# Q and K products over two pairs at a time, and a mask written over logits in PSUM, in a two-layer graph network

## The chip, the core and the metric

The kernel runs on one core of one Trainium2 chip. The time of a run is the device time of that core in microseconds, from the start of the execution to its end. The kernel before takes 2388.6 us (median of 3 runs, 2387.88 to 2389.69).

A core has five engines that run their own streams of instructions in order: PE (TensorE, matrix products, with the weight loads shown apart as PEld), DVE (VectorE), ACT (ScalarE), POOL (GpSimd) and SP (SyncE, which here issues nearly all DMAs). They wait for each other through semaphores.

## The reference

There are 128 independent batches. Each has x with 128 rows and 512 columns in float32 and a 128x128 integer adjacency. Two layers follow each other:

```python
# layer 0: attention with 8 heads of 64 columns, masked by the adjacency
q, k, v = x @ Wq + bq, x @ Wk + bk, x @ Wv + bv
logits = einsum('bqhd,bkhd->bhqk', q, k) / 8
attn = softmax(where(adj > 0, logits, -1e9))
x = layernorm(x + relu(einsum('bhqk,bkhd->bqhd', attn, v) @ Wo + bo))
# layer 1: graph attention with one head
Wh = x @ W
e = leaky_relu((Wh @ a1)[:, None] + (Wh @ a2)[None, :], 0.2)
x = layernorm(x + elu(softmax(where(adj == 0, -1e9, e)) @ Wh))
```

All of it is float32.

## The kernel before

**Pairs.** The work goes by pairs of batches: pair p holds batches 2p and 2p+1, so there are 64 pairs. Everything of a pair is a step with a name (`qk0`, `logits`, `mask_logits1`, `w_c11` and so on), a small function that emits its instructions.

**Products with a weight.** Four weights are applied: Wq and Wk (together `wqk`, their output kept with features on partitions), Wv, Wo and W. The two batches of a pair and the two halves of the contraction make a two-by-two block form, and the products are made with seven block products in place of eight (`PRODUCTS`), with sums of blocks made ahead: `weight_sums` once for each weight, `left_sums` for each pair (steps `x_sums`, `o_sums`, `z_sums`, four operations on POOL each). The seven block products accumulate in three PSUM banks A, B, C, and between them ACT or DVE read the banks and combine (steps `_p1`, `_p6`, `_c11`, `_p7`, `_c22`, `_c21`, `_c12`). For V, O and W the weight is the moving operand, 256 columns wide (`rows_product`, L531). For Q and K the weight block is stationary and x is the moving operand, 128 columns (the rows of one batch or of one sum) wide (`columns_product`, L542): 4 feature chunks by 2 contraction chunks, 8 matrix instructions for each block product. A float32 matrix instruction appears in the trace as two records on PE and two on PEld.

**Attention.** `logits(p)` (L791) makes the logits of both batches of the pair, one after the other: 8 heads each, contraction over 64 rows, two heads side by side on the two halves of the array's rows. The result of a batch fills two PSUM banks (pool `ps_att`, two buffers). POOL has filled an SBUF tile `pr` with -1e9 (`fill_logits`, L799; two buffers); DVE copies the logits over it where the mask is one (`mask_logits`, L803), which sets the PSUM buffer free, and takes the negated row maximum from `pr` (L808). ACT takes the exponential in place with its row sum (L814, 8 instructions with a reading of the accumulator each), DVE inverts the sums, ACT scales (L824), DVE transposes 32x32 blocks into `prb` (L837), and SP writes `prb` to HBM and reads it back in the other order into `prT` (L850, L859: one DMA and four). `mix_values(b)` (L869) multiplies with V: outputs of 64 partitions, two heads side by side on the two halves of the array's columns. In layer 1, `mix_nodes` (L997) multiplies the attention with x on the whole array.

**x.** `load_blocks(p)` loads both batches of a pair in 32x32-friendly order into `xb`, `x_transpose` (L586, DVE) transposes a batch into `xT` (four buffers), and `load_x` loads the plain rows for the residual (two buffers).

**The order.** Nothing is scheduled at run time. `PLAN` gives each step a due time within a pair, `PERIOD` is added for each later pair, and `ENDS` shifts steps in the first and last pairs; all steps are sorted by that time and emitted in that order, and each engine's stream is what results. Only the order counts, the times themselves are never waited for. `GOING` adds empty products (`keep_going_late`, L1086) at a few places near the end. The last pair has shorter ways: transposes on PE instead of DMA, W and O products in plain form (L713), and work on DVE that is otherwise POOL's (`side_engine`).

Of the kernel before, what the change touches and what calls it, by code (L numbers as in the profile page):

```python
# [17 lines left out]
PERIOD = 81.828156  # L18
PLAN = dict(
    load_blocks=-169.2518, sums_qk=-116.3679, sums_v=-101.8019, x_transpose0=-86.1319, x_transpose1=-79.7504,  # L20
    sums_o=-74.3987, x_sums=-35.3263, qk0=-32.7245, qk1=-27.0361, qk4=-25.8081, qk_p1=-24.9029, qk_p1q=-24.7398,
    qk_p6=-23.2631, qk2=-21.6091, qk_c11=-19.491, qk3=-17.7869, fill_logits1=-14.9084, qk_p7=-13.984,
    load_adj=-12.9311, qk_c22=-9.2149, v0=-8.4276, qk5=-7.2181, qk6=-7.1845, qk_c21=-5.2279, v_p1=-4.9633,
    fill_logits0=-4.7424, v1=-3.3064, qk_c12=-2.1207, v_p6=-1.6137, v2=-1.3636, mask=-0.6144, logits=0.0,
    mask_logits0=2.1354, v3=3.4342, v_c11=5.3342, sums_fold1=5.6709, max_logits0=7.2929, v4=7.8473, v_p7=10.5301,
    v_c22=11.0507, v5=11.2435, mask_logits1=11.7414, v6=12.2065, v_c12=13.0477, v_c21=13.7783, max_logits1=14.0311,
    exp_logits0=14.9455, sums_fold_t1=29.5382, sum_logits0=36.5851, sums_fold0=38.0441, sums_fold_out1=39.3173,
    sums_fold_t0=41.2777, norm_logits0=49.133, exp_logits1=53.5487, weights_t0=54.0334, sum_logits1=54.4411,
    norm_logits1=57.8787, sums_fold_out0=60.6355, weights_out0=64.5346, weights_t1=66.3279, weights_out1=76.2441,
    weights_in0=76.8757, mix_values0=83.0319, weights_in1=83.7749, mix_values1=84.6403, mix_values_out0=86.1105,  # L30
    mix_values_out1=88.1579, sums_w=91.2147, o_sums=95.3864, o0=95.754, load_x1=104.4976, o_p1=109.4377,
    o1=117.6112, o4=119.0515, load_x0=121.4079, o_p6=122.4978, fill_edges=124.7475, o_p1l=126.1443, o3=126.686,
    o2=130.451, o_p7=131.8715, o_c11=134.1407, o_c22=134.3039, o5=134.9475, o6=135.0912, o_c21=136.1861,
    o_c12=136.4788, residual00=137.0927, stats00=138.5041, mean00=144.6048, residual01=145.8591, stats01=147.1796,
    rstd00=149.175, mean01=149.4786, shift00=151.0198, rstd01=151.4241, norm00=152.5598, shift01=155.6025,
    norm01=156.4175, edge_term10=156.4398, edge_term11=160.2785, edge_blocks=166.4223, edge_term01=170.0896,
    edge_term00=172.7812, edge_row=180.5447, edge_sums=180.8282, edge_leaky=182.3038, edge_mask=194.0334,
    edge_max=194.7432, edge_exp=203.146, edges_t=205.2742, edges_t_out=211.9867, edges_t_in=212.3358,
    mix_nodes1=225.9448, mix_nodes_out1=227.9602, edge_norm=229.8523, mix_nodes0=230.0102, mix_nodes_out0=234.9992,
    z_sums=244.2793, w0=261.4366, w1=262.5692, w_p1=262.5723, w_p6=263.0005, w2=264.29, w3=266.6663, w_c11=267.2067,  # L40
    w4=268.1639, w_p7=273.5439, w_c22=276.1897, w5=278.0097, w_c21=278.1222, w6=279.5606, w_c12=283.7313,
    elu_exp1=292.9307, elu_exp0=299.1665, elu_low1=300.2511, elu_low0=311.7113, elu_max1=315.4258,
    elu_max0=317.7063, tail_exp=321.2554, residual10=327.3123, residual11=342.0393, stats10=351.2992,
    mean10=362.4035, stats11=364.5992, mean11=365.5761, rstd10=371.9636, shift10=402.4303, finish0=423.5343,
    rstd11=447.2308, shift11=460.7052, finish1=468.0909, store0=483.1352, store1=502.9344, tail_max=616.0679,
    tail_sum=623.954, tail_norm=855.4691)
# [3 lines left out]
        load_x0=-307.1688, qk_p1=-220.4916, qk6=-209.3085, qk5=-208.2226, x_transpose0=-184.4755,  # L50
        fill_logits0=-182.6106, qk_p1q=-177.9107, qk2=-176.9987, x_transpose1=-174.505, qk0=-168.3877,
        qk_c11=-153.0006, qk1=-151.2359, qk_c21=-146.2578, qk3=-135.3339, qk_c12=-133.7443, fill_logits1=-117.9224,
        tail_exp=-115.7058, qk_c22=-114.2801, qk4=-109.4256, mask=-96.5947, qk_p6=-95.0022, tail_max=-93.0873,
        v1=-92.9444, v0=-88.8394, logits=-85.7847, mask_logits0=-83.9035, v_p1=-82.6878, v2=-81.4129, v_p6=-81.3346,
        norm_logits0=-79.0358, max_logits0=-75.6452, x_sums=-73.0228, qk_p7=-72.4402, v3=-72.1557,
        sum_logits0=-71.2808, weights_t0=-65.6654, mask_logits1=-65.4693, v_p7=-63.2932, v4=-62.9197,
        load_adj=-62.6051, exp_logits1=-62.2906, v_c11=-60.6749, v5=-59.9717, v_c22=-57.2207, exp_logits0=-53.7987,
        max_logits1=-49.1528, finish0=-37.8374, weights_out0=-36.1445, v6=-35.9047, stats11=-34.6264,
        tail_sum=-33.7386, v_c12=-32.1388, v_c21=-30.8773, weights_in0=-29.626, store0=-26.7007, shift01=-26.6327,
        weights_in1=-25.8217, edge_term01=-24.2286, rstd01=-23.1277, stats01=-22.9131, o_c11=-22.584,  # L60
        mean01=-22.0409, residual01=-21.8677, sum_logits1=-20.5549, residual11=-20.3839, o2=-19.79,
        weights_out1=-18.3632, o_p1l=-17.629, shift10=-17.1551, o3=-17.1166, norm01=-16.4822, o_p6=-16.4536,
        o_c22=-15.7638, o_c21=-15.4619, o5=-15.3535, o_p7=-15.3253, o1=-15.1127, o4=-14.5824, elu_exp1=-13.7949,
        weights_t1=-13.7748, norm_logits1=-11.4151, o6=-11.2616, mix_values0=-10.9462, mix_values1=-10.1036,
        o_p1=-9.8975, edge_row=-9.4454, edge_mask=-9.2922, elu_low1=-9.2535, residual00=-9.2117, o_c12=-8.661,
        w_c22=-8.624, elu_max1=-7.7019, w_p7=-7.4203, mix_values_out1=-7.2999, mix_values_out0=-7.2036,
        edge_term11=-6.8813, edge_sums=-5.9449, w5=-4.9426, w_c12=-4.5009, w0=-4.39, w_p1=-4.1709, mean10=-3.9319,
        w6=-3.836, w_c21=-3.5995, w2=-3.414, w_c11=-3.3202, w1=-2.7704, load_x1=-2.4908, edge_blocks=-1.6838,
        w4=-1.5143, edges_t_out=-1.3526, o0=-1.2931, w3=-0.7222, rstd10=-0.6162, edge_term00=-0.5897, w_p6=-0.2046,
        o_sums=0.3336, edges_t=0.5007, edge_exp=1.3317, edge_leaky=2.1715, rstd00=2.3393, mix_nodes1=2.6091,  # L70
        stats10=2.6585, edge_max=2.9908, stats00=4.202, finish1=5.0102, mix_nodes_out1=5.0231, mean00=5.5742,
        edges_t_in=5.865, mix_nodes0=5.8668, shift11=6.2663, mix_nodes_out0=6.8887, edge_term10=7.4794,
# [220 lines left out]
def tile_two_graph_layers(ctx: ExitStack, tc: tile.TileContext, x, adj, wq, bq, wk, bk, wv, bv, wo, bo, w, a, out,  # L293
# [13 lines left out]
    DH = D // H  # L307
    HALF = D // 2
    n_pair = n_batch // 2
    NEG = -1.0e9  # L310
    EPS = 1e-5
    ALPHA = 0.2

# [858 lines left out]
```

## Time and profile before

| quantity | value |
| --- | --- |
| time, median of 3 | 2388.6 us |
| span of the profiled execution, first to last instruction | 2386.0 us |
| PE busy | 2365.4 us (99%), 17762 records |
| PEld busy | 2148.5 us (90%) |
| DVE busy | 1904.3 us (80%), 3891 instructions |
| ACT busy | 1539.8 us (65%), 5501 instructions |
| POOL busy | 1399.1 us (59%), 1984 instructions |
| DMA | 276 MB, mean busy share 45% of 16 engines |
| mean granted TensorE clock | 0.999 |

The span ends 2.6 us short of the median time. A busy PE means that a matrix instruction is in it; the ends of matrix instructions are modelled, so that the true rate is read from the starts of instructions that follow each other. In a timeline a row gives the start, the time from the first start to the last end, engine, line, operation, tile written and tiles read, shapes and the number of records; what is in brackets is the idle time of the engine just before and what ended it. The chain of waits is followed back from the last instruction, at each step to what released it.

### The profile page before, as it was taken

To read this page: it belongs to the slowest core of one execution; us is meant where nothing else is said; L and a number is where in the kernel's file an instruction comes from. 1 tells how busy PE (TensorE), PEld (TensorE's weight loads), DVE (VectorE), ACT (ScalarE), POOL (GpSimd) and SP (SyncE) were. 2 spreads that over 40 slices of the span, in tenths; PEclk is the share of its full clock that TensorE was granted. 3 is DMA by queue.
4 is the path that set the end of the run, shared out by engine and by line. 5 is a ranking of instruction groups with operands and counts; after the bars stand their busy time and mean duration, and the time that the engine had idled before them with its cause. 6 is when DMAs were issued, how large, how long until landed. Compare 5 with 4: busy or idle time off the path is not lost.

```text
span 2386.0 us, 51849 instructions
## 1 busy us (share of the span) xinstructions
PE 2365.4 (99%) x17762; PEld 2148.5 (90%) x17762; DVE 1904.3 (80%) x3891; ACT 1539.8 (65%) x5501; POOL 1399.1 (59%) x1984
## 2 busy tenths in 40 slices
PE   8999999999999999999999999999999999999997
PEld 8998999989989999999899999998998999989985
DVE  6778888788788887887887878878878788787787
ACT  4665676666766756666667567666675675666664
POOL 3355655656656656566566565565665655656557
PEclk9999999999999999999999999999999999999999
DMA  7444444535444445454444443443544444445342
GB/s 188 118 98 102 127 109 116 131 90 129 123 99 130 110 115 131 94 126 127 94 130 114 110 131 96 129 127 89 130 121 102 131 108 117 122 96 138 102 103 78
DMA packets 340981, 276.18 MB, mean 116 GB/s; under 512 B 126192, under 2 KB 288496, under 8 KB 340720
## 3 DMA queue, kind: packets, MB, share of 16 engines
q1 hardware_dynamic: 339504, 271.57, 45.3%
q8 instruction: 142, 2.33, 0.4%
q10 hardware_dynamic: 1216, 1.31, 0.2%
q14 instruction: 119, 0.97, 0.1%
HBM read 156.77 MB, written 107.74 MB: 111 GB/s over the span
## 4 chain that ended last, share of the span: by engine, by line
PE 95%; ACT 1%; DMA 1%; DVE 1%; POOL 1%; issue 0%; SPq 0%; POOLq 0%; ACTq 0%; DVEq 0%
PE pBqk L542 14%; PE pCqk L542 9%; PE pAqk L542 9%; PE pACw L531 9%; PE pACo L531 9%; PE pACv L531 9%; PE pBv L531 7%; PE pBw L531 7%; PE pBo L531 7%; PE s L791 5%; PE po L869 5%; PE pz L997 5%; ACT pr L814 1%; ACT pr L824 0%; DMA ejr<-ej 0%
## 5 line engine op out<-in xcount | busy, mean ns | idle before, releaser
L881 ACT ACTIVATE oT<-po,bv 128x128 f32<-128x128 f32 x508 | 146.7, 388 | 437.4 <-PE po L869 436.5
L814 ACT ACTIVATE pr<-pr,nmax 128x128 f32<-128x128 f32 x1024 | 396.4, 410 | 0.4 <-DVE nmax L808 0.4
L824 ACT ACTIVATE pr<-pr,tot 128x128 f32<-128x128 f32 x1016 | 310.6, 400 | 1.4 <-DVE tot L818 1.4
L430 POOL TENSOR_TENSOR so<-oT 128x256 f32<-128x256 f32 x63 | 45.9, 728 | 392.4 <-ACT oT L881 392.4
L1033 POOL TENSOR_SCALAR t<-t 128x512 f32<-128x512 f32 x126 | 244.0, 1951 | 26.4 <-ACT t L1029 26.0
L542 PE MATMUL pAqk<-xT,wqk 128*128 128x128 f32 x2016 | 245.8, 275 | 1.9 <-ACT e1bqk L622 1.1
L542 PE MATMUL pCqk<-sx,wqk 128*128 128x128 f32 x2016 | 245.9, 275 | 0.1
L542 PE MATMUL pBqk<-sx,wqk 128*128 128x128 f32 x2016 | 245.6, 275 | 0.0
L542 PEld LDWEIGHTS pAqk<-xT,wqk 128*128 128x128 f32 x2016 | 240.0, 192 | 5.6 <-ACT e1bqk L622 1.3
L542 PEld LDWEIGHTS pBqk<-sx,wqk 128*128 128x128 f32 x2016 | 236.2, 192 | 7.0
L542 PEld LDWEIGHTS pCqk<-sx,wqk 128*128 128x128 f32 x2016 | 235.3, 192 | 0.5 <-DVE co L781 0.3
L903 DVE SCALAR_TENSOR_TENSOR scr<-co,wa_bc 128x512 f32<-128x512 f32 x256 | 218.8, 855 | 2.7 <-ACT co L579 2.4
L814 ACT ACTIVATION_READ_ACCUMULATOR pr<-pr,nmax 128x1 f32 x1024 | 214.9, 210 | 0.0
L932 POOL MEMSET at<- 128x256 f32 x64 | 19.9, 311 | 304.1 <-DVE atb L970 304.1
L803 DVE COPY_PREDICATED pr<-mask,s 128x1024 f32<-128x1024 int32 x128 | 171.6, 1342 | 15.8 <-PE s L791 15.8
L1044 POOL TENSOR_TENSOR cw<-cw,co 128x512 f32<-128x512 f32 x126 | 162.4, 1290 | 9.5 <-DVE cw L1038 9.5
L656 DVE TENSOR_TENSOR u3qk<-pBqk,e1aqk 128x512 f32<-128x512 f32 x63 | 43.6, 692 | 149.2 <-PE pBqk L542 149.1
L837 DVE STREAM_TRANSPOSE prb<-pr 128x1024 f32<-128x1024 f32 x126 | 156.1, 1239 | 7.2 <-ACT pr L824 6.1
L570 POOL TENSOR_TENSOR rstd<-rstd,half 128x1 f32<-128x1 f32 x255 | 146.7, 575 | 21.3
L808 DVE TENSOR_REDUCE nmax<-pr 128x8 f32<-128x1024 f32 x128 | 155.1, 1212 | 0.1
L791 PEld LDWEIGHTS s<-kT,qT 64*128 64x128 f32 x2048 | 119.3, 188 | 20.8 <-DVE kT L677 17.6
L531 PE MATMUL pBv<-wv,sx 128*128 128x256 f32 x512 | 137.6, 391 | 0.0
(201 smaller groups left out, 6161.4 us busy)
## 6 DMA issues: line engine op xcount, KB each, us to landing
prd<-prb SPq DMA_DIRECT2D x126, 512.0 KB, 3.0
prT<-prd SPq DMA_DIRECT2D x504, 128.0 KB, 3.6
x<-in_x_dram SPq DMA_DIRECT2D x128, 256.0 KB, 4.0
out_dram<-cw SPq DMA_DIRECT2D x128, 256.0 KB, 3.6
xb<-in_x_dram SPq DMA_DIRECT2D x252, 128.0 KB, 4.0
adj<-in_adj_dram SPq DMA_DIRECT2D x64, 128.0 KB, 3.0
ejr<-ej SPq DMA_DIRECT2D x252, 32.0 KB, 3.8
atd<-atb SPq DMA_DIRECT2D x62, 128.0 KB, 1.8
```

The costliest lines, as they stand in the source:

```text
L531: nc.tensor.matmul(out, left_block(left, blk.pair, a_i, c), right_block(weight, b_i)[:, c, :], start=first and c == 0, stop=j in LAST and ...
L542: nc.tensor.matmul(out[:, f * P:(f + 1) * P], weight[:, b_i, c, f * P:(f + 1) * P], left_block(left, blk.pair, a_i, c), start=first and f ...
L570: nc.gpsimd.tensor_tensor(RSTD[key], RSTD[key], half, op=ALU.pow)
L791: nc.tensor.matmul(ST["s", b][:, j, hp, :], q[r, hp, :], k[r, hp, :], start=True, stop=True)
L803: nc.vector.copy_predicated(PR[b], MASK[p][:, i, :].unsqueeze(1).to_broadcast([P, H, P]), ST.pop(("s", b)).rearrange("p j h k -> p (j h) k"))
L808: nc.vector.tensor_reduce(NMAX[b], PR[b], AX.X, ALU.max, negate=True)
L814: nc.scalar.activation(PR[b][:, h, :], PR[b][:, h, :], AF.Exp, bias=nmax[:, h:h + 1], scale=1.0, accum_out=TOT[b][:, h:h + 1])
L824: nc.scalar.activation(PR[b][:, h, :], PR[b][:, h, :], AF.Copy, scale=tot[:, h:h + 1])
L837: nc.vector.transpose(PRB[b].rearrange("p k h s -> p h k s"), PR.pop(b).rearrange("p h (k r) -> p h k r", r=32))
L903: nc.vector.scalar_tensor_tensor(scr, X1[b], 1.0, wa_bc[s], op0=ALU.mult, op1=ALU.mult, accum_out=acc)
L1033: side_engine(b // 2).tensor_scalar(t, t, 1.0, -1.0, op0=ALU.min, op1=ALU.add)
L1044: side_engine(b // 2).tensor_tensor(Y[b], Y[b], X1.pop(b), op=ALU.add)
```

## The change

**Quads.** The outer unit becomes a quad g of two pairs (`n_quad` = 32), with a `PERIOD` and a `PLAN` for a quad. In 30 of 32 quads a Q/K product takes the rows of both pairs as one moving operand of 256 columns (`qk_product`, L799 after): for each half h of the features (`qk0..`, `qk1..`), 7 block products of 2 feature chunks by 2 contraction chunks. The combining steps keep their width of 512, but ACT's take two instructions of 256 columns in place of four of 128 (`with_bias`). The first and the last quad keep products by pair (`by_pair`).

**x.** `xT` becomes two constant tiles with three slots, a ring of three pairs (`slot`, `both`, `turn`); sums of x are made for both pairs at once in four tiles `sx`. `xb` holds one batch (three buffers instead of two of two batches). `x` has one buffer instead of two.

**Mask.** The mask is inverted, and DVE writes -1e9 (a constant tile `neg`, broadcast) over the logits in PSUM where there is no edge. The row maximum and the exponential read PSUM, and the exponential writes `pr`, which has one buffer instead of two. `fill_logits` goes. The PSUM buffer is free after the exponential.

**Order.** `logits`, `mix_values` and all others are placed by batch; `logits` is called for one batch. `PLAN` and `ENDS` are new, `ENDS` replaces due times instead of shifting them, `GOING` goes, loads of Wo, W, bo and a are placed by the plan, and `side_engine` gives DVE the work of the last two pairs.

```diff
-PERIOD = 81.828156
+PERIOD = 71.920000
 PLAN = dict(
...
-    load_adj=-12.9311, qk_c22=-9.2149, v0=-8.4276, qk5=-7.2181, qk6=-7.1845, qk_c21=-5.2279, v_p1=-4.9633,
-    fill_logits0=-4.7424, v1=-3.3064, qk_c12=-2.1207, v_p6=-1.6137, v2=-1.3636, mask=-0.6144, logits=0.0,
...
+    load_adj0=41.0709, qk1_c21=41.2501, qk1_c12=42.8115, logits00=44.2929, mask0=44.8618, mask_logits00=45.5151,
+    max_logits00=46.8321, logits01=47.0309, exp_logits00=48.1659, mask_logits01=49.5631, v00=51.5747,
...
+    v0_p6=54.4487, v03=55.0581, v0_p7=56.1580, v0_c11=56.7433, v05=56.8342, weights_t00=56.9264, v04=57.7010,
+    exp_logits01=58.2992, v0_c22=58.9343, weights_out00=59.2192, v06=59.4458, v0_c21=59.5343, v0_c12=60.6158,
+    sum_logits01=62.1660, norm_logits01=62.5609, weights_in00=63.4812, weights_t01=65.5665, logits10=66.4329,
+    weights_out01=67.0077, load_adj1=68.6031, mix_values00=69.1731, weights_in01=71.1015, mix_values_out00=71.9175,
+    mask1=72.5812, v11=73.5829, mask_logits10=74.3575, v10=74.4474, mix_values01=75.3150, v1_p1=75.7529, v12=76.2653,
+    v1_p6=76.8054, logits11=77.1295, mix_values_out01=77.1569, max_logits10=78.0202, v13=78.1206, v1_c11=78.7230,
...
+def by_pair(g):
+    return g == 0 or g == n_quad - 1
...
+XT.update((r, const.tile([P, 3, NC, P], F32, tag=f"xT{r}", name=f"xT{r}")) for r in range(2))
...
+def both(g):
+    return (slice(0, 2), slice(0, 3, 2), slice(1, 3))[g % 3]
...
+def qk_product(g, h, j):
...
+    feats = range(NC) if by_pair(g) else range(2 * h, 2 * h + 2)
+    width = D // len(feats)
+    for n, f in enumerate(feats):
+        for c in range(2):
+            left = x_block(g, a_i, c)
+            to = out[:, n * width:(n + 1) * width]
+            nc.tensor.matmul(to if by_pair(g) else to.rearrange("p (u n) -> p u n", n=P),
+                             wqk[:, b_i, c, f * P:(f + 1) * P], left[:, turn(2 * g + h)] if by_pair(g) else left,
...
-def logits(p):
-    for b in (2 * p, 2 * p + 1):
-        q, k = (QK[m, b].rearrange("r (h n) -> r h n", n=P) for m in "qk")
-        ST["s", b] = ps_att.tile([P, 2, H // 2, P], F32, tag="att", name=f"s_{b}")
-        for hp in range(H // 2):
-            for j in range(2):
-                r = slice(j * DH, (j + 1) * DH)
-                nc.tensor.matmul(ST["s", b][:, j, hp, :], q[r, hp, :], k[r, hp, :], start=True, stop=True)
+def logits(b):
+    ST["s", b] = ps_att.tile([P, 2, H // 2, P], F32, tag="att", name=f"s_{b}")
+    for hp in range(H // 2):
+        for j in range(2):
+            r = slice(j * DH, (j + 1) * DH)
+            nc.tensor.matmul(ST["s", b][:, j, hp, :], qk_operand("q", b, hp)[r], qk_operand("k", b, hp)[r],
+                             start=True, stop=True)
...
-def fill_logits(b):
-    PR[b] = buf([P, H, P], F32, "pr", f"pr_{b}")
-    nc.gpsimd.memset(PR[b], NEG)
-def mask_logits(p, i):
-    b = 2 * p + i
-    nc.vector.copy_predicated(PR[b], MASK[p][:, i, :].unsqueeze(1).to_broadcast([P, H, P]),
-                              ST.pop(("s", b)).rearrange("p j h k -> p (j h) k"))
+def mask_logits(b):
+    nc.vector.copy_predicated(flat_logits(b), MASK[b // 2][:, b % 2, :].unsqueeze(1).to_broadcast([P, H, P]),
+                              neg.unsqueeze(2).to_broadcast([P, H, P]))
...
 def exp_logits(b):
+    PR[b] = buf([P, H, P], F32, "pr", f"pr_{b}")
...
-        nc.scalar.activation(PR[b][:, h, :], PR[b][:, h, :], AF.Exp, bias=nmax[:, h:h + 1], scale=1.0,
+        nc.scalar.activation(PR[b][:, h, :], s[:, h, :], AF.Exp, bias=nmax[:, h:h + 1], scale=1.0,
...
-    at=1, xb=2, adj=3, so=1, xT=4, sx=1, qT=2, kT=2, pr=2, e1a256=2, u2256=1, mask=1, cv=2, u3256=1, scr=1, cw=6,
-    prb=1, e1a512=1, e1b512=1, u2512=1, u3512=1, prT=2, oT=2, x=2, e1b256=2, co=6, ejr=1, e=1, atb=2, attT=1, zT=2,
-    sz=1, t=2)
+    at=1, xb=3, adj=3, so=1, sx=4, qT=4, kT=4, pr=1, e1a256=2, u2256=1, mask=1, cv=2, u3256=1, scr=1, cw=4, prb=1,
+    e1a512=1, e1b512=1, u2512=1, u3512=1, prT=2, oT=2, x=1, e1b256=2, co=6, ejr=1, e=1, atb=2, attT=1, zT=2, t=2)
```

## The prediction

> **What bounds the kernel now.** I read the page from the top: the span, the busy shares, then the chain of waits.
>
> ```profile
> span 2386.0 us, 51849 instructions
> ...
> PE 2365.4 (99%) x17762; PEld 2148.5 (90%) x17762; DVE 1904.3 (80%) x3891; ACT 1539.8 (65%) x5501; POOL 1399.1 (59%) x1984
> ...
> PE 95%; ACT 1%; DMA 1%; DVE 1%; POOL 1%; issue 0%; SPq 0%; POOLq 0%; ACTq 0%; DVEq 0%
> ```
>
> PE is busy all along and 95% of the chain is PE. A change to DVE, ACT or POOL is worth nothing by itself here; what counts is how long PE takes for its own stream, and whether anything starts to make it wait. So I went to PE's timeline in a steady pair and read the starts.
>
> ```profile
> 1005.42 1.03 PE L531 MATMUL pBo<-wo,so 128*128 128x256 f32 x4
> ...
> 1023.96 1.95 PE L542 MATMUL pCqk<-sx,wqk 128*128 128x128 f32 x16
> 1025.75 1.03 PE L531 MATMUL pBv<-wv,sx 128*128 128x256 f32 x4
> 1026.62 1.03 PE L531 MATMUL pACv<-wv,xT 128*128 128x256 f32 x4
> 1027.57 2.06 PE L791 MATMUL s<-kT,qT 64*128 64x128 f32 x32
> 1029.56 1.97 PE L869 MATMUL po<-prT,cv 128*64 128x128 f32 x32
> 1031.46 1.13 PE L531 MATMUL pBv<-wv,sx 128*128 128x256 f32 x4
> 1032.42 1.03 PE L531 MATMUL pACv<-wv,sx 128*128 128x256 f32 x4
> 1033.29 1.03 PE L531 MATMUL pBv<-wv,xT 128*128 128x256 f32 x4
> ...
> 1042.00 1.03 PE L531 MATMUL pBo<-wo,so 128*128 128x256 f32 x4
> ```
>
> The same product recurs after 36.58 us: the period of a pair, 73.16 for two pairs. Sixteen records of 128 columns take 1.786 (1023.96 to 1025.75), 0.1116 us each; four of 256 take 0.8635 (1032.42 to 1033.29 and its like), 0.2159 each. Two things follow.
>
> First, 256 columns cost 1.93 times what 128 do: a Q/K instruction (two records) is 0.2232 us at 128 columns and 0.4318 at 256, so pairing saves 0.0146 us for each wide one.
>
> Second, logits (s) and value mixing (po) cost more than their streams. They run two small instructions side by side, so 32 records are 16 steps: 1.786 us at 0.1116 (s) and 1.744 at 0.109 (po, from starts within it). The four intervals around them are 0.95 (pACv before s), 1.99, 1.90 and 0.96 (pBv after po). Over 0.8635, 1.786, 1.744 and 0.8635 that is 0.09+0.20+0.155+0.10, or 0.545 us lost for one visit of s and po. Is it a wait for k? An earlier pair tells:
>
> ```profile
> 110.42 1.03 PE L531 MATMUL pACv<-wv,xT 128*128 128x256 f32 x4
> 111.29 1.03 PE L531 MATMUL pBv<-wv,sx 128*128 128x256 f32 x4
> 112.25 2.06 PE L791 MATMUL s<-kT,qT 64*128 64x128 f32 x32
> ...
> 109.73 0.69 DVE L677 TENSOR_TENSOR kT<-pCqk,u2qk 128x512 f32<-128x512 f32 x1 [0.21 <-PE pCqk L542]
> ```
>
> Here k was written by 110.42, 1.8 us before s starts, and pBv still takes 0.96. It is the change of the array's shape.
>
> **What the Trainium skill says.** "TensorEngine Tiling (Array Packing)", Key Properties: "Changing tiling mode (not just tile) drains the TensorE". The trace agrees: about 0.1 us on each side of each change. "TensorE: Matmul & The Clock Gate", Step-by-step: what each phase is for, says that weight loads are pulled ahead of running products; the trace shows loads beside products in full-array runs, and the first weight load of s at the start of s itself. "VectorE: DVE Perf Modes", Why PSUM operands drop a tier: float32 in PSUM runs at the single rate. Agrees: 692 ns for a 512-wide addition with a PSUM operand (u3qk), 682 without (residual). Its Specifications put ScalarE closer to PSUM: a 128x128 ACTIVATE takes 353 ns from PSUM (e1aqk), 410 from SBUF (the exponential).
>
> **The change, part by part.**
>
> Q and K: in the built order 1680 wide instructions replace 3360 narrow ones; 1680 x 0.0146 = 24.5 us saved.
>
> Logits and mixing by batch: in the order of the changed program nearly each of the 128 + 128 visits stands alone between full-array products, as pBw, s, pACw, s, pACw, po, pACw. Before: 64 entries from the full array to s, 63 passages s to po, so 64 joint visits. After: 124 entries to s, 121 to po, 10 passages between them; that is 117 lone s, 118 lone po, 10 joint. A lone s costs 0.09+0.20+0.10 = 0.39: this occurs once before, at 23.85 to 27.76 us of the timeline, 0.96, 1.98 and 0.97 us in place of 0.8635, 1.786 and 0.8635. A lone po is seen without its entry (1.03 and 0.97 in place of 0.872 and 0.8635, 0.26); with 0.09 for the entry, 0.35. After: 117 x 0.39 + 118 x 0.35 + 10 x 0.545 = 92; before 64 x 0.545 = 35. Added: 57 us. This is what decides.
>
> Mask: the DVE copy of 1342 ns now writes PSUM. No row shows that form. Lower end: 1.2 us, the 1024-wide reduction; upper: double, 2.7. I take 1.34, since both stream 1024 elements through DVE. Even double adds 5.4 us to DVE's 59.0 of 73.2 in two pairs: 64.4 of 74, still beside PE. The maximum from PSUM stays near 1.21, the exponential gets some 50 ns x 8 cheaper. The fill (121 us of POOL) goes; POOL was idle 41%. Half of the Q/K bias instructions go from ACT, idle 35%. All are worth nothing under PE's cover; uncovered they would only take load off.
>
> x: the same bytes in twice as many loads on SP. Before, SP issues about 28 DMAs a pair at 0.4 to 0.65 us, some 14 of 36.6 us; four more are 2 us, hidden. With one x buffer, the second load waits for the first residual, and the second residual is due 3.9 us after that load with 4.0 to land: DVE waits a few tenths, and products queued behind it on PE have that much less slack. I take 0.2 us for a quad.
>
> One pr buffer: a batch holds it for 3.1 (exponentials) + 0.2 + 2.4 (scaling) + 1.24 (transpose), about 7 us, four times in 74. The tightest way on is batch 1 of a quad. The plan has its transpose end at 66.8 and its mixing on PE at 75.3, 8.5 apart. The rows:
>
> ```profile
> prd<-prb SPq DMA_DIRECT2D x126, 512.0 KB, 3.0
> prT<-prd SPq DMA_DIRECT2D x504, 128.0 KB, 3.6
> ```
>
> 3.0 out, then four issues at 0.5 to 0.65 before the last starts (1.5 to 1.95), 3.6 to land and 0.4 of handing on: 8.5 to 8.95. It misses by 0 to 0.45, but a lone s and a lone po lie between on PE and make it 0.6 later than the plan thinks. I take no more than 0.1.
>
> Ends: PE's stream by these durations is 2346 us before, without the empty products, and 2378 after. Of the span 40 lie outside: 6.4 before the first product, 8.1 after the last, 5 of empty products, about 5 of waits at the start, 9 in the last 80 us, and 0.09 a pair in the middle. The new ends put 65 us of PE work behind the last logits, in place of 57, where 11.5 were idle: the tail can take up about 4 us of the added work. At the start, batches 2 and 3 are needed sooner, with sums on POOL: 0 to 5 us lost. I take 0 for both together.
>
> Sum, per profiled execution: 2386.0 - 24.5 + 57 + 30 quads x 0.15 (4.5) = 2423. The median stands 2.6 above the span: 2425.6, say 2425.
>
> **The rivals.**
>
> Faster: the loss of a visit does not multiply, since in the changed order other waits fall into it or a lone visit of small operands drains less. Place: before and after each s and po. The change breaks even when a lone visit costs (35 + 24.5) / 245 = 0.24 us, against my 0.35 to 0.39; at nothing added it gives 2364. For: in the steady pairs k ends only 0.08 us before s, so a part might have been a wait. Against: 0.96 at 112.25, with k long there. 0.06.
>
> Slower still, by a new wait: the weights' way through one pr buffer, SP and HBM. The prT load has taken up to 4.8 us to land; at 1.2 late in every quad, with what DVE and ACT then hand on late, PE waits 1 to 1.5 us a quad: 2455 to 2470. Speaks for it: the 8.5 above. Against: PE is itself 2 us a quad later than the plan. 0.16. DVE as the bound is part of this size: it needs a masked copy above 6 us.
>
> Half the price: waits of before that vanish (0.09 a pair, 5 us) and ends that save 10: 2405 to 2412. 0.13.
>
> **How the numbers follow.** The main case, 2412 to 2442, has 0.63; with the milder and the lower part of the heavier case 2402 to 2458 holds 8 in 10. A change below 0.2% (4.8 us) could not be told from none. Faster 0.06, same 0.02, slower 0.92.
>
> **What would show it.** In the changed profile: wide Q/K records 0.216 us apart; two pairs in 74.0 to 74.5 us; each lone s or po with a row before and after it 0.1 us longer than its like; PE still about 98% busy and over 90% of the chain; DVE near 80%. If two pairs take below 73 us, the lone visits are cheaper than I say; if above 75, look for PE waits on prT or on DVE in the list of waits. The masked copy's row above 2 us would make the second rival likelier.

## The result, and the profile after

The changed kernel takes 2447.7 us (median of 4 runs, 2445.58 to 2449.91), beside 2388.2 for the kernel before on the same chip. The ratio is 1.025, with a 95% interval from 1.0236 to 1.0265. It is slower, by 59.5 us where I had said 36: outside the main case of the prediction (2412 to 2442) and inside its wider range (2402 to 2458).

The page of the changed kernel, its head:

```profile
span 2443.8 us, 44946 instructions
...
PE 2399.6 (98%) x14358; PEld 2031.0 (83%) x14358; DVE 1892.6 (77%) x3895; ACT 1484.0 (61%) x5141; POOL 1336.9 (55%) x1733
```

PE has 3404 records fewer and is busy 34 us longer. Every other engine has less to do than before. The span grew by 57.8.

The page's chain of waits can't be read here: it was followed back over a few per cent of the span only. So I go by PE's timeline, a steady quad, with the columns as before:

```profile
1001.99 1.03 PE L731 MATMUL pBo<-wo,oT 128*128 128x256 f32 x4
1002.94 1.16 PE L1001 MATMUL s<-kT,qT 64*128 64x128 f32 x16
1004.04 1.13 PE L731 MATMUL pACw<-w,zT 128*128 128x256 f32 x4
1005.00 1.03 PE L731 MATMUL pBw<-w,sz 128*128 128x256 f32 x4
1005.96 1.09 PE L1080 MATMUL po<-prT,cv 128*64 128x128 f32 x16
1006.98 1.13 PE L731 MATMUL pBw<-w,sz 128*128 128x256 f32 x4
...
1028.70 1.89 PE L799 MATMUL pBqk<-sx,wqk 128*128 128x256 f32 x8
1030.43 1.89 PE L799 MATMUL pAqk<-xT,wqk 128*128 128x256 f32 x8
...
1077.04 1.16 PE L1001 MATMUL s<-kT,qT 64*128 64x128 f32 x16
```

Three readings. Eight wide Q/K records take 1.73 us (1028.70 to 1030.43), 0.216 each. A lone s has 0.95 before it, 1.10 for itself and 0.96 after it, where the streams alone are 0.8635, 0.893 and 0.8635: 0.39 lost. And the same s comes back after 74.10 us, where 74.0 to 74.5 was forecast.

Is the loss a wait for data after all? The page has a row for the weight loads of these products: after the bar stand the busy time, the mean of one in ns, and the idle time before them with what ended it. The first row is from the kernel before, the other two from the changed one:

```profile
L791 PEld LDWEIGHTS s<-kT,qT 64*128 64x128 f32 x2048 | 119.3, 188 | 20.8 <-DVE kT L677 17.6
...
L1001 PEld LDWEIGHTS s<-kT,qT 64*128 64x128 f32 x2048 | 124.2, 187 | 41.5 <-issue 39.3
L1080 PEld LDWEIGHTS po<-prT,cv 128*64 128x64 f32 x2048 | 109.4, 136 | 44.2 <-issue 40.3
```

"Issue" is idle time for which the profile shows nothing that was waited for. Before, most of the idle time at the 64 entries to s was put down to kT, 0.33 us each. After, it is the same third of a microsecond at 120 entries to s, and nothing is named. So the loss is there without any wait for data on record.

**The balance.** I took from the starts of PE's instructions what their streams and the changes of shape account for (0.1116 and 0.2159 us a record, the prices of the prediction), and call the rest waits; empty products count there too, and so does what products lose at a lower clock.

| us | before | after | difference |
| --- | --- | --- | --- |
| streams and changes of shape | 2342.3 | 2374.4 | +32.1 |
| waits, 0 to 100 us | 13.4 | 11.0 | -2.4 |
| waits, 100 to 400 | 1.4 | 13.4 | +12.0 |
| waits, 400 to 2000 | 4.4 | 2.4 | -2.0 |
| waits, 2000 to 2300 | 1.1 | 12.9 | +11.8 |
| waits, 2300 to the last product | 13.9 | 15.9 | +2.0 |
| after the start of the last product | 8.4 | 12.6 | +4.2 |
| first product's start | 1.2 | 1.2 | 0 |
| span | 2386.0 | 2443.8 | +57.8 |

The first row was forecast as 57 - 24.5 = 32.5. It is reckoned with the prediction's own prices, so it shows that the records and visits are those that were counted, not that the prices are right. That is seen in the middle, where these prices leave almost nothing over: it has fewer waits than before, not more. The other 26 us are at both ends, in the quads that have an order of their own. The list of PE's waits from 95 to 420 us (engine, waiting tile and line, releaser: us in total, times, longest) of the kernel before has one row:

```profile
PE pACw L531 <- DVE cw L766: 0.2, 1, 0.2
```

and of the changed kernel ten, of which the first three are

```profile
PE pBw L731 <- DVE qT L881: 2.2, 2, 1.9
PE po L1080 <- DMA prT<-prd: 1.6, 1, 1.6
PE pBqk L799 <- DVE u3qk L867: 1.3, 1, 1.3
```

Some of the rest at the ends is the clock. In the trace of the changed kernel the granted clock is at half from 2403.0 to 2406.4 us. The first row gives a stretch, its length, the busy time of PE, PEld, DVE, ACT and POOL, the granted clock, the DMA share and GB/s; the others are PE's timeline:

```profile
2403.10:2406.30 3.20, 3.20 (x11) 2.56 (x10) 3.06 (x8) 0.76 (x4) 2.83 (x5) 0.50 0.40 136
...
2404.27 1.91 PE L731 MATMUL pBw<-w,sz 128*128 128x256 f32 x4
2405.98 1.29 PE L1207 MATMUL pz<-attT,co 128*128 128x128 f32 x8
```

Four records of 256 columns take 1.71 us there (2404.27 to 2405.98) in place of 0.8635. By the starts of its products PE loses 1.5 us in this stretch; the trace of before has no such stretch ahead of its last product. Other traces below have several, outside the middle only, so that a few us between two traces can be this. The kernel before makes empty products near its end, which the change dropped; whether they would keep the clock up was not run.

The groups of instructions settle the mask. The first two rows are from the kernel before:

```profile
L814 ACT ACTIVATE pr<-pr,nmax 128x128 f32<-128x128 f32 x1024 | 396.4, 410 | 0.4 <-DVE nmax L808 0.4
L803 DVE COPY_PREDICATED pr<-mask,s 128x1024 f32<-128x1024 int32 x128 | 171.6, 1342 | 15.8 <-PE s L791 15.8
...
L1025 ACT ACTIVATE pr<-s,nmax 128x128 f32<-128x128 f32 x1024 | 360.1, 378 | 136.4 <-DVE prb L1048 73.1
...
L1012 DVE COPY_PREDICATED s<-mask,neg 128x1024 f32<-128x1024 int32 x128 | 162.5, 1270 | 19.8 <-PE s L1001 19.5
L1017 DVE TENSOR_REDUCE nmax<-s 128x8 f32<-128x1024 f32 x128 | 155.6, 1216 | 1.1
```

The masked copy into PSUM takes 1270 ns on the mean, 72 less than the one out of it (1342). The exponentials keep ACT busy for 360.1 us in place of 396.4, 35 ns less for each of 1024 (some 50 were forecast). They overlap on ACT: from one start to the next it is 343 ns after and 385 before (medians). In the run with the mask part alone it is 360.2 us and 342 ns, so that this comes from reading PSUM and not from the new order.

### The profile page after: what moved, and what is told of

Read it like the earlier page. It is cut to its first block, busy times and chain, and to the rows that moved or that the text cites. A ratio compares the mean times of both kernels' runs of the same rounds, so it can differ in the third digit from the quotient of the medians.

```text
span 2443.8 us, 44946 instructions
## 1 busy us (share of the span) xinstructions
PE 2399.6 (98%) x14358; PEld 2031.0 (83%) x14358; DVE 1892.6 (77%) x3895; ACT 1484.0 (61%) x5141; POOL 1336.9 (55%) x1733
## 5 line engine op out<-in xcount | busy, mean ns | idle before, releaser
L1025 ACT ACTIVATE pr<-s,nmax 128x128 f32<-128x128 f32 x1024 | 360.1, 378 | 136.4 <-DVE prb L1048 73.1
L799 PE MATMUL pBqk<-sx,wqk 128*128 128x256 f32 (+1 forms) x1056 | 241.6, 372 | 0.7 <-DVE mv L751 0.6
L799 PE MATMUL pCqk<-sx,wqk 128*128 128x256 f32 (+1 forms) x1056 | 238.6, 370 | 1.8 <-POOL sx L588 1.8
L799 PE MATMUL pAqk<-xT,wqk 128*128 128x256 f32 (+1 forms) x1056 | 238.7, 370 | 0.0
L756 POOL TENSOR_SCALAR rstd<-mv 128x1 f32<-128x1 f32 x255 | 62.9, 247 | 309.2 <-DVE mv L751 290.5
L1025 ACT ACTIVATION_READ_ACCUMULATOR pr<-s,nmax 128x1 f32 x1024 | 221.7, 216 | 0.0
L799 PEld LDWEIGHTS pCqk<-sx,wqk 128*128 128x128 f32 x1056 | 193.7, 190 | 27.0 <-POOL sx L588 2.0
L799 PEld LDWEIGHTS pBqk<-sx,wqk 128*128 128x128 f32 x1056 | 189.5, 190 | 31.5 <-issue 4.1
L799 PEld LDWEIGHTS pAqk<-xT,wqk 128*128 128x128 f32 x1056 | 193.4, 190 | 25.2
L1012 DVE COPY_PREDICATED s<-mask,neg 128x1024 f32<-128x1024 int32 x128 | 162.5, 1270 | 19.8 <-PE s L1001 19.5
L1001 PEld LDWEIGHTS s<-kT,qT 64*128 64x128 f32 x2048 | 124.2, 187 | 41.5 <-issue 39.3
L1017 DVE TENSOR_REDUCE nmax<-s 128x8 f32<-128x1024 f32 x128 | 155.6, 1216 | 1.1
L1001 PE MATMUL s<-kT,qT 64*128 64x128 f32 x2048 | 148.5, 285 | 0.4 <-ACT pr L1025 0.4
L1080 PEld LDWEIGHTS po<-prT,cv 128*64 128x64 f32 x2048 | 109.4, 136 | 44.2 <-issue 40.3
```

Source lines behind the costliest of these rows:

```text
L799: nc.tensor.matmul(to if by_pair(g) else to.rearrange("p (u n) -> p u n", n=P), wqk[:, b_i, c, f * P:(f + 1) * P], left[:, turn(2 * g + h) ...
L1001: nc.tensor.matmul(ST["s", b][:, j, hp, :], qk_operand("q", b, hp)[r], qk_operand("k", b, hp)[r], start=True, stop=True)
L1012: nc.vector.copy_predicated(flat_logits(b), MASK[b // 2][:, b % 2, :].unsqueeze(1).to_broadcast([P, H, P]), neg.unsqueeze(2).to_broadcast( ...
L1017: nc.vector.tensor_reduce(NMAX[b], flat_logits(b), AX.X, ALU.max, negate=True)
L1025: nc.scalar.activation(PR[b][:, h, :], s[:, h, :], AF.Exp, bias=nmax[:, h:h + 1], scale=1.0, accum_out=TOT[b][:, h:h + 1])
```

## The experiments

Theory at the outset: PE pays by the change of the array's shape, so narrow products and lone visits are what moves the time. A visit is a run of small products (s or po) between products on the whole array. It is lone when one batch's s or po stands by itself, and joint when s and po follow each other. A product is called cover for another engine when that engine reads a bank while the product runs. In what follows "period" is the mean distance between recurring starts of value mixing on PE, for two pairs, over some 1100 us of the middle. It tells the middle from the ends, which the time alone doesn't.

| kernel | period, us | time, us |
| --- | --- | --- |
| before | 73.20 | 2388 |
| mask part alone, in before | 73.20 | 2395.7 |
| one product between s and po, in before | 75.00 | 2437.6 |
| all visits lone, in before | 78.76 | 2538.1 |
| after | 74.11 | 2447.7 |
| narrow Q/K | 74.95 | 2472.2 |
| visits in two groups | 75.20 | 2484.8 |
| visits in three groups | 73.92 | 2454.9 |
| two joins of two | 74.01 | 2452.6 |
| mixing on the whole array | 76.38 | 2519.7 |

**Narrow Q/K products in the changed kernel.**

```diff
-nc.tensor.matmul(to.rearrange("p (u n) -> p u n", n=P), wqk[...], left, ...)
+for u in range(2):
+    nc.tensor.matmul(to[:, u * P:(u + 1) * P], wqk[...], left[:, u], ...)
```

> The changed kernel with each 256-column Q/K instruction of the 30 wide quads made as two of 128 columns, one for each pair, on the same weight block; nothing else. Theory (a wide instruction saves 0.0146 us): 1680 x 0.0146 = 24.5 us more, so 2472 us, and two pairs in 74.10 + 0.82 = 74.9 us. Rival (weight loads hide behind products either way, so width is worth nothing): 2448, 74.1.

Measured: 2472.2 us (ratio 1.0348, 1.0333 to 1.0363), 24.5 over the changed kernel. The period grew by 0.84, and 56 wide instructions a quad at 0.0146 are 0.82. So the gain of the wide products was there in full, and was spent elsewhere. The period is the firmer figure: that the whole time also meets the forecast to the microsecond is in part chance, since PE loses nearly 7 us in stretches at half clock in this trace, against 1.5.

**Value mixing on the whole array.** It is the test of the cause.

```diff
-nc.tensor.matmul(ST["o", b][j * DH:(j + 1) * DH, hp, :], v[:, h * DH:(h + 1) * DH],
+nc.tensor.matmul(ST["o", b][:, hp, :], v[:, hp * P:(hp + 1) * P],
```

> The changed kernel with value mixing made on the whole array: each head is multiplied with the 128 V columns of its pair of heads and writes all 128 output partitions, so that the second head of a pair overwrites the first (this leaves out the half of the mixing that the first head gives, and the other half carries the wrong head beside it). Same operands, same buffers, same waits, same order; only the shape of the array does not change any more for a po. Theory (the change of shape is what costs): the rows beside a po lose their 0.1 us, and a po takes 16 records x 0.1116 = 1.79 us for its 16 products in place of 0.872 + 0.35; that is +0.57 for each of 128, +72 us, 2520. Rival (the 0.35 is a wait for prT or for the output bank, whatever the shape): the rows beside po stay 0.1 long and the price of 0.35 comes on top, +0.92 for each, +117 us, 2565. The s visits stay as they are in both.

Measured: 2519.7 us (one run), against 2520 and 2565. The period grew by 2.27; four times 0.57 is 2.28. The timeline of that kernel:

```profile
1001.64 1.89 PE L799 MATMUL pCqk<-sx,wqk 128*128 128x256 f32 x8
1003.37 1.95 PE L1080 MATMUL po<-prT,cv 128*128 128x128 f32 x16
1005.15 1.89 PE L799 MATMUL pBqk<-sx,wqk 128*128 128x256 f32 x8
1006.88 1.89 PE L799 MATMUL pAqk<-xT,wqk 128*128 128x256 f32 x8
```

The rows before and after po are 1.73 like any of their kind, and po takes 1.78 for 16 records: nothing is lost at its edges. With the same tiles, buffers and order the 0.35 us is gone. In this trace the weight loads of po are idle for 3.8 us with nothing named, in place of 40.3; those of s, whose shape still changes, for 38.8 in place of 39.3. For po it is thus the change of shape and no wait for data. No run made s on the whole array; for s the cause is inferred from the same pattern and the same idle weight loads. (The mixing as a whole is dearer, since its two small products no longer run side by side.)

**One product between logits and mixing, in the kernel before.** Only v3 moves, in 55 of 64 pairs.

```diff
+SPLIT = dict(v3=1.0)
...
-events.append((p * PERIOD + PLAN[key] + shift, len(events), fn, args))
+due = SPLIT.get(key, PLAN.get(key)) if middle(p) else PLAN[key]
+events.append((p * PERIOD + due + shift, len(events), fn, args))
```

> The kernel before with one V product (v3) moved between the logits and the value mixing in 55 of its 64 pairs, so that s po becomes s pBv po; no other step moves. Theory (price of a change of shape): leaving s 0.197 and entering po 0.145 in place of 0.15 from s to po, +0.19 a pair, +10.6 us: 2399. Rival (a joint visit is as dear as two single ones, or the price is a wait that v3 would cover): 2387 to 2390. Rival (po, later by one product, makes others wait): 2405 or more.

Measured: 2437.6 us (1.0205, 1.019 to 1.022), 49 more, in place of 10.6. The period of a pair grew by 0.90. Its timeline says why:

```profile
1011.58 2.06 PE L793 MATMUL s<-kT,qT 64*128 64x128 f32 x32
1013.56 1.13 PE L533 MATMUL pBv<-wv,sx 128*128 128x256 f32 x4
1014.62 1.97 PE L871 MATMUL po<-prT,cv 128*64 128x128 f32 x32
1017.22 1.13 PE L533 MATMUL pACv<-wv,sx 128*128 128x256 f32 x4 [0.63 <-ACT cv L756]
```

The 1.06 from pBv to po is 0.8635 and the 0.2 of a second change of shape, as forecast. But v3 had stood between po and v4, and while it ran, ACT had read bank A into cv. ACT writes cv here 0.2 us after po has ended (1016.78, against 1016.6), and the next product, which writes the tile being read, waits for it; that cv's buffer comes free with po is my reading of it (ACT's own order, with this copy behind outputs of po, would give the same). The second rival, that others are made to wait, came true beside the price. I had looked for the price of the moved product and not for what it covered where it had stood.

**All four visits of a pair alone, in the kernel before.**

```diff
+SPLIT = dict(
+    logits0=0.0, v3=0.5, logits1=0.7, v4=1.0, mix_values0=PERIOD + 1.2037, v_p7=1.5, v5=2.0,
+    mix_values1=PERIOD + 2.8121)
```

> The kernel before, with s and po of the 55 middle pairs set apart by one V product each (v2 s v3 s v4 po v5 po v6) in place of v2 s s po po v3; nothing of the change is in it. Theory: (2 x 0.39 + 2 x 0.35 - 0.545) = 0.935 us a pair, 55 x 0.935 = 51, so 2440 us and 37.5 us a pair. Rival (visits do not add up by themselves): 2388 to 2393.

Measured: 2538.1 us (1.0623, 1.0607 to 1.0639). A pair grew by 2.78 us. Two lone s and two lone po cost 2 x 0.39 + 2 x 0.35 - 0.545 = 0.935 more than a joint visit; the other 1.84 are new waits, from the list of PE's waits between 1000 and 1300 us:

```profile
PE pACw L535 <- ACT e1aw L730: 6.6, 7, 0.9
PE pACv L535 <- DVE cv L770: 4.8, 8, 0.6
```

One for each pair of the 300 us, 0.9 and 0.6. The list counts from the modelled end of the product before, which lies up to 0.17 us behind the start of the next (1.03 against 0.8635); with that for each, the two make up the 1.84. Same lesson.

**The visits of the changed kernel in two groups a quad** ([s s po po], twice).

```diff
+PLAN.update(
+    logits00=47.0303, logits01=47.0309, mix_values10=118.9512, mix_values11=118.9515, mix_values_out10=120.3,
+    mix_values_out11=121.6, mask_logits00=48.10, max_logits00=49.42, exp_logits00=50.75, mask_logits01=50.76,
+    mix_values00=75.3147, mix_values01=75.3150, logits10=75.3153, logits11=75.3156, mix_values_out00=76.5,
+    mix_values_out01=77.66, mask_logits10=78.45, max_logits10=79.77)
```

> The changed kernel with the due times of logits and value mixing moved so that in the 25 middle quads they stand in two visits of four (s s po po, and po po s s) in place of eight lone ones; masks, maxima and exponentials of two batches moved with them. Theory (a lone s costs 0.39 us and a lone po 0.35 beyond its stream, a joint visit 0.53 to 0.55): 2.96 - 1.08 = 1.9 us less a quad, 25 x 1.9 = 47, so 2401 us; two pairs in 72.2 us if the moved steps cause no wait. Rival (the loss sits in the mask, the buffers or the order of DVE, and visits cost nothing): 2448 or more, since the moved steps come up to 9 us later than planned.

Measured: 2484.8 us (1.0398, 1.038 to 1.0415). Two joint visits in place of eight lone ones take 2.96 - 1.09 = 1.87 us off a quad, to 72.2. The period is 75.20, so that 3.0 us of waits came in. These three, 1.9 us a quad by the list, are the larger part:

```profile
PE pACw L737 <- DVE cw L984: 2.7, 4, 0.7
PE pBw L737 <- POOL sz L597: 2.7, 4, 0.7
PE pACv L737 <- DVE cw L999: 2.2, 4, 0.5
```

Each comes once a quad. The W products that a visit had stood between now follow each other at once, and wait for DVE to read their banks and for POOL to make their sums. The time then also rose at the ends, where steps placed by this plan lie between the others.

**Three groups, with two W products moved to keep their cover.** Here c22 reads bank C after product 6 and not before it, so that in the steady quads a quarter of W's output for one pair of the two is a wrong sum; instructions and tiles are the same.

```diff
+PLAN.update(
+    logits00=47.0303, logits01=47.0309, mix_values10=118.9512, mix_values11=118.9515, ...
+    logits10=69.1730, logits11=75.3153, w05=193.6822, w06=194.5497, w0_c22=194.74, w0_c21=194.90, w0_c12=195.63,
+    o10=123.42)
```

> The changed kernel with its visits grouped again in the steady quads, three visits in place of eight ([s s po po], [s po], [po s]), and two W products moved so that none of the steps that come between two readings of a bank lose their cover. Theory (price by visit): 1.35 us a quad less, in 25 quads 34 us: 72.75 us a quad and 2414. Rival (grouping always uncovers waits on DVE and POOL, as in the first grouping): 74 us a quad or more, 2440 to 2480.

Measured: 2454.9 us (1.028, 1.0265 to 1.0296). The price of three joint visits (1.64) puts the period at 72.78; it is 73.92, and 1.14 us are waits, 0.43 of them this one:

```profile
1070.95 1.13 PE L737 MATMUL pACv<-wv,xT 128*128 128x256 f32 x4 [0.43 <-DVE cw L999]
```

So the middle gained 0.19 a quad, and the ends lost more than that.

**Two joins only** (a lone s beside a lone po, twice a quad).

```diff
+PLAN.update(logits10=69.1730, logits11=75.3153)
```

> The changed kernel with two of a quad's eight visits put beside another (logits10 next to mix_values00, logits11 next to mix_values01), the rest as it is; six visits a quad in place of eight. Theory (price by visit): 0.39 + 0.35 - 0.545 = 0.2 us each, 0.4 a quad, in 25 quads 10 us less: 2438. Rival (each joint uncovers a wait for a bank): 2447 or more, with a new wait of PE of 0.1 to 0.6 in every quad.

Measured: 2452.6 us (1.0258, 1.0244 to 1.0272), not to be told from the changed kernel: the intervals overlap. Of 0.39 us a quad 0.10 came through (74.11 to 74.01). The list of waits from 500 to 1700 us has a new one, of a weight load, once in each of 16 quads:

```profile
PEld pBw L733 <- POOL sz L591: 7.0, 16, 0.4
```

The rival was right. At the ends PE loses 9.9 us in stretches at half clock in this trace, against 1.5, which is more than the gain of the middle (25 x 0.1 us). Taken together: a lone visit costs 0.35 to 0.39 us on PE, but in this kernel it also gives DVE, ACT and POOL time to hand on a bank, and three quarters of its price or more came back as waits when it went.

**The mask part alone, in the kernel before** (inverted mask, -1e9 written over the logits in PSUM, no fill, everything else as it was).

```diff
-nc.vector.copy_predicated(PR[b], MASK[p][...].to_broadcast([P, H, P]), ST.pop(("s", b))...)
+nc.vector.copy_predicated(flat_logits(b), MASK[p][...].to_broadcast([P, H, P]), neg...to_broadcast([P, H, P]))
```

> The kernel before with the mask alone changed: the mask inverted, -1e9 written over the logits in PSUM, maximum and exponential read from PSUM, no fill; two pr buffers and the old order stay. Theory (all of it lies under PE): 2388, within 3 us, with the masked copy near 1.25 us and POOL some 120 us less busy. Rival (the longer hold of the logits' PSUM or DVE's PSUM writes stall PE): 2395 to 2410.

Measured: 2395.7 us (1.0026, 1.0016 to 1.0037), 7 more. The period is that of before, so in the middle the mask part is worth nothing either way. The loss is in the first 100 us, where PE's waits are 19.2 us and not 13.4 (1.6 of the difference is a stretch at half clock, 52.4 to 55.9 us):

```profile
PE pwa L496 <- DVE wa_rep L490: 4.0, 2, 3.3
PE pBv L533 <- DVE u3v L763: 2.5, 1, 2.5
```

In the kernel before these two tiles wait 0.3 us (there on ACT) and 0.6. That the longer hold of the PSUM buffers puts DVE late there is argued, not shown. The changed kernel has another order at the start and waits less there (11.0).

**The side engine in the last pair only, in the changed kernel.**

```diff
-return nc.vector if p >= n_pair - 2 else nc.gpsimd
+return nc.vector if p == n_pair - 1 else nc.gpsimd
```

> The changed kernel with the work of the side engine on DVE only in the last pair, as before, not in the last two. Theory (the ends lose by the order of many small hand-ons, no single edit does it): within 3 us of the changed kernel, 2445 to 2451, and PE's waits between 2000 and 2300 us stay at about 13 us. Rival (DVE is overloaded in the last quad by this edit, and that makes the tail): 4 to 8 us faster, 2440 to 2444.

Measured: 2452.8 us (1.0269, 1.0252 to 1.0287). Neither: 5 us above the changed kernel at the median, though the intervals of the two ratios just overlap. In its trace the last product starts 2 us later, and PE loses 2.3 us more at half clock, so that this part says nothing of the edit. After the start of the last product 16.7 us follow, where 12.6 do after the change. So this edit of the change, if anything, helps the tail.

**The ends: a wait moved.** What are the 26 us? One of the larger waits, on the timeline of the changed kernel (several engines):

```profile
306.34 0.69 ACT L1151 ACTIVATE e<-ejr,ei 128x128 f32<-128x128 f32 x2 [3.47 <-DMA ejr<-ej]
306.94 0.82 ACT L827 ACTIVATE qT<-pAqk,bqs 128x256 f32<-128x256 f32 x2
...
309.44 0.45 DVE L1180 STREAM_TRANSPOSE atb<-at 128x256 f32<-128x256 f32 x1 [0.94 <-ACT at L1169]
309.85 0.67 DVE L881 SCALAR_TENSOR_TENSOR qT<-pBqk,e1bqk 128x512 f32<-128x512 f32 x1
310.67 1.10 PE L731 MATMUL pBw<-w,sz 128*128 128x256 f32 x4 [1.88 <-DVE qT L881]
```

PE waits for bank B, which DVE reads into qT. That step stands on DVE behind a transpose of layer 1 (atb), which waits for ACT; and ACT had stood 3.47 us before the DMA that brings the neighbours' terms (ejr). The releaser that the wait names is the last of a chain. So I moved edge_sums, and in two places what follows it, behind the steps that PE needs.

```diff
+ENDS[1].update(edge_sums1=185.2000, edge_leaky1=185.2003, edge_mask1=185.2006, edge_max1=185.2009, edge_exp1=185.2012,
+               edges_t1=185.2015)
+ENDS[2].update(edge_sums1=184.2000, edge_leaky1=185.1003, edge_mask1=185.1006, ..., edge_norm1=185.1018)
+ENDS[-4].update(edge_sums1=190.5000)
+ENDS[-3].update(edge_sums0=127.5000)
+ENDS[-1].update(edge_sums0=107.9000)
```

> The changed kernel with the steps edge_sums (and in two places the steps on DVE after it) of five pairs in the end orders moved later, behind the oT, zT and qT steps that now stand behind them on ACT or DVE while edge_sums waits for the DMA of ejr. Nothing else moves. Theory (the waits at the ends are made by the written order: a step that waits for a DMA stands ahead of one that PE needs): the waits at 228, 246 to 308, 2246, 2255 and 2397 us, 2.0 + 0.65 + 0.94 + 2.3 + 3.0 = 8.9 us, go, and 5 to 9 us with them: 2439 to 2443. Rival (the layers' chains at the ends are themselves too long, and PE meets the same delay a little later): 2446 to 2450.

Measured: 2452.8 us (1.0265, 1.0251 to 1.0279): no gain. The waits at 308 and 2397 us are gone, and in the list of waits from 95 to 420 us others stand in their place:

```profile
PE s L1009 <- DVE kT L896: 2.8, 2, 2.1
PE po L1088 <- DMA prT<-prd: 2.4, 2, 1.7
```

PE's waits are 62.5 us in all, in place of 55.6. Nearly all of this difference lies in stretches at half clock: PE loses 8.1 us in four of them (a wait of 0.75 among it), against 1.5 in the one of the changed kernel. Without them the two are alike, 54.4 and 54.1. Moving the chain in the order only moves where PE meets it.

**The ends: DVE relieved, or the chain shortened**, each in the seven quads with an order of their own.

```diff
 def mask_logits(b):
+    if b // 4 < 3 or b // 4 >= n_quad - 4:
+        return
```

> The changed kernel without the masked copy (1.27 us of DVE) in the first three and the last four quads, the ones that have an order of their own; 28 batches go unmasked there (this leaves out the mask for them), which takes 36 us from DVE. Theory A (DVE's load makes the waits of PE at the ends): PE's waits outside 400 to 2000 us, 54 us after the changed kernel's own count, fall by a third or more: 10 to 18 us faster, 2430 to 2438. Theory B (the ends wait for chains that go through DMAs and several engines, not for DVE's throughput): 0 to 5 us faster, 2443 to 2448.

```diff
 ej = EJ.pop(p)
+if p // 2 < 3 or p // 2 >= n_quad - 4:
+    nc.gpsimd.memset(ST["j", p], 0.0)
+    return
 for v in range(4):
     nc.sync.dma_start(ST["j", p][:, v, :], ...)
```

> The changed kernel with the four DMAs of ejr replaced by one memset of the same tile on POOL in the first three and the last four quads (this leaves out the neighbour's term of layer 1's logits there). It takes some 2.4 us of issues and 3.7 us of landing out of layer 1's chain at the ends, and nothing else. Theory B1 (the chain of layer 1 through this DMA is what PE meets at the ends): the waits at 228, 308, 2246, 2255 and 2397 us, 8.9 us, go and stay gone, 6 to 9 us faster, 2438 to 2442. Theory B2 (as with edge_sums moved: what is taken from one wait is met by the next, since the ends are short of work that is ready for PE): 2444 to 2450.

Measured: 2444.3 us (1.0233, 1.0218 to 1.0248) with 36 us of DVE's work gone, and 2435.0 us (1.0196, 1.0179 to 1.0213) with the DMA gone. The first is 4 us shorter in its span and its interval overlaps that of the changed kernel: DVE's load is not what makes most of the waits. The chain through the DMA is a large part of it. In the second kernel PE's waits are 42.2 us, 13.4 less, and the span is 13.5 shorter (12.7 by the medians), more than the 8.9 that I had put to this chain. Of the 13.4, 1.5 are the stretch at half clock, which this trace does not have ahead of its last product. The same list from 95 to 420 us begins with

```profile
PE pBo L731 <- DVE cv L987: 1.0, 2, 0.6
PE pBo L731 <- DVE tot L1029: 0.7, 1, 0.7
```

and neither qT nor a DMA for prT is in it. That prT comes in time too says that SP's 2.4 us of issues may have a part beside the landing; this kernel takes both away, and doesn't tell them apart.

Some 12 to 13 us of the ends are thus shown to go with layer 1's row DMA and its issues. The same cut in the kernel before was not run; its waits from 100 to 400 and from 2000 to 2300 us, 2.5 in all, leave it little to gain there. Another 13 us stay open. 4.2 of them lie behind the start of the last product, where the run without the DMA has 12.5 us as well. A second buffer for x or for pr, which would have told whether these buffers have a part in it, was not tried. Nor was the plan of the middle tried in the end quads. No version that I ran beats the kernel before.

## Why the prediction was right in kind and short in size

**Right: what bounds the kernel, and the price of a visit.** The prices leave 2.4 us of 1600 over in the middle of the changed kernel, and the period is 74.10 us, forecast 74.0 to 74.5. Two runs test them one by one. Mixing on the whole array takes the loss at the edges of po away (76.38 us a quad, forecast from the price 76.39), and narrow Q/K products lengthen a quad by 0.84 us (forecast 0.82). The rival "faster", that the price doesn't multiply, is out: each lone visit pays it. The Trainium skill's sentence from "TensorEngine Tiling (Array Packing)", Key Properties, that changing the tiling mode drains TensorE, fits what po on the whole array shows; the size, 0.35 to 0.39 us for one lone visit, is the trace's.

**Right: the mask, the Q/K bias instructions.** The masked copy was taken at 1.34 us with bounds of 1.2 and 2.7; it is 1.27. DVE is at 77%, forecast near 80. The mask alone leaves the middle at 73.20 us. At the start of the kernel before it cost 7 us, which "worth nothing under PE's cover" had not: there PE waits for DVE in the first 52 us. One reading beside these was no test: the additions of 692 and 682 ns, with and without a PSUM operand, are nearly alike, so they show neither a drop of rate nor its absence.

**Too high: x and pr with one buffer each.** The sum has 0.15 us a quad for them, 4.5 in all, though its terms read 0.2 and up to 0.1; that is a slip. PE's waits from 400 to 2000 us fell from 4.4 to 2.4. With one pr buffer ACT does wait, 73.1 us in all before the exponentials (the row of L1025), but the list of PE's waits from 1000 to 1300 us is empty. The second rival, 1 to 1.5 us of waits a quad on the way of the weights, is out with it.

**Wrong: "I take 0 for both together".** This is the step that failed, the term for the ends. I had let a tail that was idle for 11.5 us take up 4 us and the start lose 0 to 5. Measured: 100 to 400 us +12.0, 2000 to 2300 us +11.8, and 4.2 more after the last product. The mistake in it: I counted how much work the new ends put on PE and what idle time was there to take it, but did not follow the chains of the end orders, where a step waits for a DMA with others behind it that PE needs. Taking that DMA away gave 13.4 us back. Taking 36 us of work from DVE there gave 4.0 us of span. I also looked at the first batches and the last 80 us only, while seven quads of 32 have orders of their own. About half of the loss at the ends is not explained by this and stays open.

**Luck.** The time lies between the main case (up to 2442) and the second rival (from 2455), and the wider range holds it because it was drawn to take in the lower part of that rival. That rival's cause, the way of the weights, did not occur; the ends filled its place.

**Not to be tested:** PE's share of the chain of waits, since the page's chain broke off.

## What to carry to other kernels

Count the entries into another array shape, not only the columns: here each lone visit of small products cost what 24 to 27 pairings of a weight block saved. When a product is moved, ask what was being read while it ran where it stood; in every regrouping tried, the cover that went cost at least three quarters of what the visits saved (0.29 of 0.39 us, 1.14 of 1.33, 3.0 against 1.87). And a change that brings its own order for the first and last rounds must be costed there by chains, wait by wait; what holds for the steady state says nothing about it.

## What the runs showed of the hardware

A masked copy with a constant, broadcast operand that writes 1024 elements a partition over PSUM takes 1.27 us (1.30 in the kernel before with the mask part), a little less than the copy from PSUM to SBUF at 1.34.

A product of 64 output columns on half of the array and its twin beside it take 0.109 us for the pair of records; one record on the whole array with the same rows takes 0.1116. Side by side the mixing needs half of the stream (0.87 against 1.78 us for a batch); the 0.91 us saved are well above the 0.35 us that the change of shape costs.

An exponential of 128x128 in float32 with its row sum follows the one before after 343 ns when it reads PSUM and after 385 ns when it reads SBUF; with the mask part alone in the kernel before it is 342.

In these traces of one core the granted clock fell to half for stretches of 3.4 us, or twice that, at the ends: ahead of the last product once in the changed kernel, four times with edge_sums moved, and not in the kernel before. Each 3.4 us cost PE about 1.5 us.
